# A convolutional LSTM over image diagonals followed by a small circuit layer: first statistics shared by ScalarE and Pool, the waiting rows' bias as a matmul, and diagonals declared apart from other rows

## The chip, the cores and the metric

One Trainium2 chip, one core of it. The metric is the device time of one execution in microseconds (us); the kernel before takes 1460.05 us, the median of three runs (1458.62 to 1461.36). A profiled execution adds a trace of every instruction of the engines: TensorE (PE, with its weight loads as PEld), VectorE (DVE), ScalarE (ACT), Pool (GpSimd), and the DMA queues (SP's above all).

## What is computed

The input x is 16 images of 128 channels, 64 by 64. Two layers, each with a group normalisation ahead of it and a residual around it:

```python
x = x + diagonal_lstm(group_norm(x), w_is, b_is, w_ss, b_ss)
x = x + circuit(group_norm(x), pre_w, pre_b, q_weights, post_w, post_b)

# diagonal_lstm: row i of an image is shifted right by i, so that column t of the shifted image is
# a diagonal. The scan goes over the 127 columns; all 64 rows at once, one state (h, c) per row.
gates = w_is @ xs[t] + w_ss[:, :, 0] @ h_of_the_row_above + w_ss[:, :, 1] @ h + b
o, f, i = sigmoid(gates[0:3]);  g = tanh(gates[3])
c = f * c + i * g;  h = o * tanh(c)          # h is the output for this column
```

A row whose pixels have not begun still moves on: its input is zero, and its state, the same for all images, follows from the bias and the row above. Group normalisation takes mean and variance over four channels and all pixels of an image. The second layer is per pixel: four angles from the channels, sines, amplitudes of a 4-qubit circuit, four expectations, 128 outputs.

## The kernel before

Channels lie on the 128 partitions. The kernel has three stages.

**Preparation (L220 to L430).** For each image b, `rows(b)` and `behind(b)` start the DMAs of x on SP's queue: 40 of the 64 rows go into `ring`, which stays, the other 24 into seven passing buffers. `statistics(b, k)` (L285) takes bn_stats of a chunk of 512 pixels on VectorE, eight for each image, and `aggregated(b)` (L289) joins them by bn_aggr into mean and variance `mv1`. Beside that runs the recursion of the waiting rows, `inv_step` (L191), 33 steps one after the other: four matmuls of the summed weights wsT with hinv (L199), four activations with the gate's bias (L202), two products and a sum on Pool (L205 to L207), a tanh (L209) and the product with the output gate (L210), which gives the next hinv. After each step come two matmuls by `keep` (L179), whose results nobody reads. The loop over b (L375) writes down, for each image, some two steps, then the image's DMAs, then its statistics. After it, Pool copies hinv into the scan's first state (L402, L403), TensorE multiplies it (L408) and runs three more `keep`s, the group mean and inverse root are made, and the scan's first product (L583) follows. `turned` and `coefficients` (L300, L312) make the circuit's coefficients with a sine on ScalarE and small Pool operations, early in this stage.

**Scan (L501 to L890).** 160 steps. The 64 rows are taken as 32 slots in two bands: band 0 is rows 0 to 31, band 1 follows 65 steps later with rows 32 to 63. `step(t)` (L753) multiplies on TensorE: for the state's sums and differences (L763), and `gate_ps(t + 1)` (L576) the normalised input of the next step (L583). VectorE adds (L778), ScalarE activates (L782, L842), VectorE makes the new state (L848). Pool makes the differences of neighbouring rows (`differences`, L614 and L617), adds the state of the step before to x in `ring` (`residual`, L627), and normalises the diagonal of step t + 2 (`normalised`, L564, L569, L574). Each diagonal is an access pattern over `ring` that touches one pixel of each active row in all images, so that its extent spans nearly the whole ring. `statistics(us)` (L703) takes bn_stats of finished rows on VectorE for the second layer's normalisation, as many as fit the given time. When four rows 4g to 4g + 3 are finished, with g below 6, they are stored to DRAM (`low`, L639); when their statistics are taken too, four later rows are reloaded in their place (L722). Within a step the order written is: products, statistics, residual of t - 1, normalising of t + 2, gates. Dependencies between engines and DMAs are found from the tiles and extents that instructions read and write, and turned into semaphore waits.

**Second layer (L947 to L1122).** Per image and chunk: angles, sines, amplitudes, outputs, and the store.

The order on each engine is the order in which the code is written (`manual_schedule`).

## Time and profile before

| | |
|---|---|
| median of three runs | 1460.05 us |
| the profiled execution | 1460.57 us |
| its span in the profile | 1458.5 us |
| PE busy | 1368.0 us (94%) |
| DVE busy | 972.0 us (67%) |
| POOL busy | 887.0 us (61%) |
| ACT busy | 776.8 us (53%) |
| mean granted TensorE clock | 0.982 |

The page gives busy times by engine, the span in 40 slices, the DMA queues, the chain of work that ended last, and the costliest groups of instructions. By time: the preparation lasts to about 103 us, the scan to about 1331 us, the second layer to the end. A wait is shown as the idle time of an engine ahead of an instruction and what released it ("<-POOL spare L617"). In a timeline a line begins with the start in us and the duration, and "x8" means that eight instructions are merged.

### The profile page before, as it was taken

To read this page: it belongs to the slowest core of one execution; us is meant where nothing else is said; L and a number is where in the kernel's file an instruction comes from. 1 tells how busy PE (TensorE), PEld (TensorE's weight loads), DVE (VectorE), ACT (ScalarE), POOL (GpSimd) and SP (SyncE) were. 2 spreads that over 40 slices of the span, in tenths; PEclk is the share of its full clock that TensorE was granted. 3 is DMA by queue.
4 is the path that set the end of the run, shared out by engine and by line. 5 is a ranking of instruction groups with operands and counts; after the bars stand their busy time and mean duration, and the time that the engine had idled before them with its cause. 6 is when DMAs were issued, how large, how long until landed. Compare 5 with 4: busy or idle time off the path is not lost.

```text
span 1458.5 us, 20029 instructions
## 1 busy us (share of the span) xinstructions
PE 1368.0 (94%) x6046; PEld 974.5 (67%) x6046; DVE 972.0 (67%) x2541; ACT 776.8 (53%) x1852; POOL 887.0 (61%) x1599
## 2 busy tenths in 40 slices
PE   6788999999999999988888899999999999999995
PEld 4668877776677766655555577767776677886332
DVE  7963555566665667765555667766666557776996
ACT  4555666555555555544444455555555556654331
POOL 4226777776677767566556577777777666763310
PEclk9999999999999999999999999999999999999998
DMA  9950000000000000323332200000000000003999
GB/s 341 407 199 1 2 1 1 1 0 1 1 1 1 1 0 1 116 73 101 116 116 86 87 0 1 1 1 1 1 1 1 0 1 1 1 30 120 362 404 355
DMA packets 64075, 107.04 MB, mean 73 GB/s; under 512 B 5040, under 2 KB 32720, under 8 KB 63968
## 3 DMA queue, kind: packets, MB, share of 16 engines
q1 hardware_dynamic: 59328, 94.39, 17.9%
q0 software_dynamic: 3408, 10.58, 2.0%
q8 instruction: 48, 0.79, 0.2%
q10 hardware_dynamic: 1232, 0.80, 0.2%
q14 instruction: 59, 0.48, 0.1%
HBM read 59.61 MB, written 46.14 MB: 73 GB/s over the span
## 4 chain that ended last, share of the span: by engine, by line
PE 77%; DVE 4%; DMA 3%; POOL 3%; issue 1%; ACT 1%; DVEq 0%; ACTq 0%; SPq 0%; POOLq 0%
PE ps L763 44%; PE ps L583 26%; DMA ring<-in_x_dram 3%; PE po_None L1042 3%; PE theta_None L991 2%; PE am_None L1020 1%; POOL ring L627 1%; DVE spare L848 1%; DVE stats L715 1%; DVE ps L838 1%; POOL spare L574 1%; DVE ps L778 1%; POOL spare L569 1%; DVE cst L841 0%; ACT g L842 0%
## 5 line engine op out<-in xcount | busy, mean ns | idle before, releaser
L583 PE MATMUL ps<-spare,wxT 128*128 128x512 f32 (+18 forms) x1280 | 479.6, 517 | 0.6 <-POOL spare L574 0.6
L778 DVE TENSOR_TENSOR ps<-ps,both 128x256 f32<-128x256 f32 (+9 forms) x536 | 219.9, 410 | 355.5 <-PE ps L763 350.2
L782 ACT ACTIVATE ps<-ps,bias 128x512 f32<-128x512 f32 (+23 forms) x480 | 279.3, 583 | 264.7 <-DVE ps L778 228.9
L763 PE MATMUL ps<-spare,w0T 128*128 128x256 f32 (+16 forms) x1272 | 352.3, 359 | 35.1 <-POOL spare L617 35.1
L763 PE MATMUL ps<-spare,w1T 128*128 128x256 f32 (+16 forms) x1272 | 353.2, 360 | 9.4 <-DVE spare L739 5.0
L583 PEld LDWEIGHTS ps<-spare,wxT 128*128 128x128 f32 x1280 | 231.1, 190 | 173.3 <-issue 155.5
L627 POOL TENSOR_TENSOR ring<-ring,spare 128x256 f32<-128x256 f32 (+15 forms) x375 | 231.7, 645 | 103.8 <-DMA ring<-in_x_dram 56.2
L813 ACT COPY both<-ps 128x256 f32<-128x256 f32 (+9 forms) x536 | 189.8, 356 | 181.8 <-PE ps L763 162.3
L763 PEld LDWEIGHTS ps<-spare,w0T 128*128 128x128 f32 x1272 | 234.8, 194 | 60.3 <-POOL spare L617 37.7
L763 PEld LDWEIGHTS ps<-spare,w1T 128*128 128x128 f32 x1272 | 234.8, 194 | 38.3 <-DVE spare L848 6.9
L763 PEld LDWEIGHTS ps<-spare,wsT 128*128 128x128 f32 x1088 | 196.3, 190 | 79.1 <-DVE spare L848 30.0
L763 PE MATMUL ps<-spare,wsT 128*128 128x256 f32 (+14 forms) x1088 | 243.9, 366 | 1.6 <-DVE spare L848 1.1
L574 POOL TENSOR_TENSOR spare<-spare,rstd 128x512 f32<-128x512 f32 (+10 forms) x160 | 171.0, 1069 | 14.7 <-DVE rstd L158 2.3
L569 POOL TENSOR_TENSOR spare<-ring 128x256 f32<-128x256 f32 (+13 forms) x165 | 140.1, 849 | 0.0
L842 ACT ACTIVATE g<-cst 128x256 f32<-128x256 f32 (+20 forms) x320 | 102.9, 368 | 64.8 <-DVE cst L841 64.3
L848 DVE TENSOR_TENSOR spare<-g,ps 128x256 f32<-128x256 f32 (+17 forms) x319 | 105.3, 368 | 43.2 <-ACT g L842 40.2
L564 POOL TENSOR_TENSOR spare<-ring,mean 128x256 f32<-128x256 f32 (+15 forms) x191 | 123.0, 644 | 5.6 <-DVE mean L148 5.4
L617 POOL TENSOR_TENSOR spare<-spare 128x240 f32<-128x240 f32 (+9 forms) x136 | 102.5, 754 | 33.6 <-DVE spare L848 29.8
L782 ACT ACTIVATE g<-ps,bias 128x512 f32<-128x512 f32 (+20 forms) x160 | 97.4, 609 | 31.0 <-DVE ps L778 24.7
L841 DVE TENSOR_TENSOR cst<-cst,ps 128x256 f32<-128x256 f32 (+20 forms) x320 | 104.6, 368 | 5.5
L838 DVE TENSOR_TENSOR ps<-ps,g 128x512 f32<-128x512 f32 (+20 forms) x160 | 95.0, 594 | 18.4 <-ACT g L782 18.3
L830 DVE TENSOR_TENSOR cst<-cst,ps 128x512 f32<-128x512 f32 (+20 forms) x160 | 92.8, 580 | 16.4 <-POOL spare L607 10.8
(370 smaller groups left out, 1015.7 us busy)
## 6 DMA issues: line engine op xcount, KB each, us to landing
out_dram<-ring SPq DMA_DIRECT2D x93, 256.0 KB, 5.1
ring<-in_x_dram SPq DMA_DIRECT2D x32, 512.0 KB, 7.3
low<-ring SPq DMA_DIRECT2D x6, 2048.0 KB, 7.5
ring<-in_x_dram SPq DMA_DIRECT2D x6, 2048.0 KB, 8.1
spare<-in_x_dram SPq DMA_DIRECT2D x27, 256.0 KB, 6.4
rest<-in_x_dram SPq DMA_DIRECT2D x21, 256.0 KB, 6.4
ring<-low POOLq DMA_DIRECT2D x18, 256.0 KB, 6.6
ring<-in_x_dram SPq DMA_DIRECT2D x16, 256.0 KB, 7.1
```

The costliest lines, as they stand in the source:

```text
L564: nc.gpsimd.tensor_sub(by_pairs(xn, 0, j0, j1), x0, over(mean1, j1 - j0))
L569: nc.gpsimd.tensor_sub(by_pairs(xn, 1, j0, j1), lower, of)
L574: nc.gpsimd.tensor_mul(v, v, r)
L583: nc.tensor.matmul(ps[g][:, :, a:b], lhsT=wxT[:, g * 128 : (g + 1) * 128], rhs=xns[t % 2][:, :, a:b], start=t > 0, stop=True, skip_group_c ...
L627: engine.tensor_add(x1, x1, by_pairs(new, q, j0, j1))
L763: nc.tensor.matmul(out, lhsT=w[:, g * 128 : (g + 1) * 128], rhs=rhs, start=False, stop=True, skip_group_check=True,)
L778: nc.vector.tensor_add(v, v, both[g][:, a:b])
L782: nc.scalar.activation(to[:, :, a:w], ps[g][:, :, a:w], FUNC[g], bias=bias[:, g : g + 1])
L813: nc.scalar.copy(both[g][:, a:b], ps[g][:, 0, a:b])
L838: nc.vector.tensor_mul(ig, ig, act[GG][:, :, a:w])
L841: nc.vector.tensor_add(c[:, q], c[:, q], ig[:, q])
L848: nc.vector.tensor_mul(new[:, q, a:v], th[:, q, a:v], act[GO][:, q, a:v])
```

## The change

Three things. First, for images 1 to 4 one of the eight chunks is no longer taken by bn_stats: ScalarE makes its sum and its sum of squares (`moments_of`), and for images 1 to 12 bn_aggr is replaced by small Pool operations for four images together (`gathering`), of which one or two are written down after each step of the waiting rows (`some`), and the rest after the loop. Second, `inv_step` puts the bias into PSUM by a matmul with the identity, adds the four products in the same bank, and activates three gates at once; the two `keep`s in the loop go, and the coefficients, with their sine, move behind the loop. Third, in the scan the diagonals' reads and adds are declared to have no dependency on the statistics, stores and reloads of other rows (`apart`, `ahead_of`); a band-1 diagonal that reaches the reloaded rows keeps its dependency on the reload.

```diff
@@ -26,6 +26,7 @@
 BLOCK = ROWS * NW
 CHUNK = 2 * BLOCK
 EARLY = 33
+GATHER = 4
...
-        def inv_step(j, pool):
-            ps = {}
-            rhs = hinv[:, j : j + 1].to_broadcast([P, P])
-            for g in ORDER:
-                ps[g] = pool.tile([P, P], F32, name=f"inv_ps{j}_{g}", tag=f"inv{g}")
-                w = wsT[:, g * 128 : (g + 1) * 128]
-                nc.tensor.matmul(ps[g], lhsT=w, rhs=rhs, start=True, stop=True)
+        def inv_step(j, pool, ident):
+            ps = pool.tile([P, 4, P], F32, name=f"inv_ps{j}", tag="inv")
+            of = bias.unsqueeze(2).to_broadcast([P, 4, P])
+            nc.tensor.matmul(ps, lhsT=ident, rhs=of, start=True, stop=False, skip_group_check=True)
+            for g in (GO, GF, GI, GG):
+                nc.tensor.matmul(
+                    ps[:, g],
+                    lhsT=wsT[:, g * 128 : (g + 1) * 128],
+                    rhs=hinv[:, j : j + 1].to_broadcast([P, P]),
+                    start=False,
+                    stop=True,
+                    skip_group_check=True,
+                )
             ac = small.tile([P, 4], F32, name=f"inv_a{j}", tag="inv_a")
-            for g in ORDER:
-                nc.scalar.activation(ac[:, g : g + 1], ps[g][:, 0:1], FUNC[g], bias=bias[:, g : g + 1])
+            nc.scalar.activation(ac[:, GO:GG], ps[:, GO:GG, 0], AF.Sigmoid)
+            nc.scalar.activation(ac[:, GG : GG + 1], ps[:, GG, 0:1], AF.Tanh)
...
             ps_prep = prep_ps.enter_context(tc.tile_pool(name="ps_prep", bufs=2, space=PSUM))
-            ps_inv = prep_ps.enter_context(tc.tile_pool(name="ps_inv", bufs=1, space=PSUM))
-            ps_keep = prep_ps.enter_context(tc.tile_pool(name="ps_keep", bufs=1, space=PSUM))
+            ps_inv = prep_ps.enter_context(tc.tile_pool(name="ps_inv", bufs=2, space=PSUM))
...
+            entries = stats[:, :, 0:8].rearrange("p b g (h s) -> p b (g h) s", s=3)
+            aside = range(1, 1 + GATHER)
+            sums1 = w_amp[:, 1, 0 : 2 * NB].rearrange("p (k i) -> p k i", i=NB)
+            gathered, within = (
+                w_amp[:, 0, k * P // 2 : (k + 1) * P // 2].rearrange("p (i e) -> p i e", i=GATHER)
+                for k in range(2)
+            )
+            def moments_of(b):
+                at = place(SLOTS)
+                v, x0 = ring[:, b, at : at + CHUNK], ring[:, b, at : at + 1]
+                junk = ps_small.tile([P, CHUNK], F32, name=f"junk{b}", tag="small")
+                for k, func in enumerate((AF.Identity, AF.Square)):
+                    nc.scalar.activation(
+                        junk, v, func, bias=x0, scale=-1.0, accum_out=sums1[:, k, b : b + 1]
+                    )
+                nc.scalar.activation(
+                    entries[:, b, 0:2, 1],
+                    sums1[:, 0, b : b + 1].to_broadcast([P, 2]),
+                    AF.Identity,
+                    bias=x0,
+                    scale=-1.0 / CHUNK,
+                )
+            def gathering(b0):
+                b1 = b0 + GATHER
+                pair = [P, GATHER, 2]
+                means, inners = entries[:, b0:b1, :, 1], entries[:, b0:b1, :, 2]
+                s1, s2 = (sums1[:, k, b0:b1] for k in range(2))
+                if b0 in aside:
+                    nc.gpsimd.tensor_mul(s1, s1, s1)
+                    nc.gpsimd.tensor_scalar_mul(s1, s1, -0.5 / CHUNK)
+                    yield
+                    nc.gpsimd.tensor_scalar_mul(s2, s2, 0.5)
+                    nc.gpsimd.tensor_add(
+                        inners[:, :, 0:2], *(v.unsqueeze(2).to_broadcast(pair) for v in (s1, s2))
+                    )
+                    yield
+                m, var = (mv1[:, b0:b1, k] for k in range(2))
+                def total(to, v):
+                    n = 8
+                    while n > 1:
+                        nc.gpsimd.tensor_add(gathered[:, :, 0:n], v[:, :, 0:n], v[:, :, n : 2 * n])
+                        v, n = gathered, n // 2
+                        yield
+                    nc.gpsimd.tensor_add(to.unsqueeze(2), v[:, :, 0:1], v[:, :, 1:2])
+                    nc.gpsimd.tensor_scalar_mul(to, to, 1.0 / 16)
+                    yield
+                yield from total(m, means)
+                nc.gpsimd.tensor_sub(gathered, means, m.unsqueeze(2).to_broadcast([P, GATHER, 16]))
+                nc.gpsimd.tensor_mul(gathered, gathered, gathered)
+                yield
+                nc.gpsimd.tensor_scalar_mul(within, inners, 1.0 / BLOCK)
+                nc.gpsimd.tensor_add(gathered, gathered, within)
+                yield
+                yield from total(var, gathered)
             q3 = qw.rearrange("p (n a) -> p a n", a=3)
+            warm = small.tile([P, 1], F32, name="warm0", tag="inv_t")
...
@@ -307,9 +374,10 @@
                 nc.gpsimd.tensor_scalar_mul(ang[:, 1], ang[:, 1], 1.0 / (4.0 * math.pi))
                 nc.gpsimd.tensor_scalar(rnd, ang, ROUND, ROUND, ALU.add, ALU.subtract)
                 nc.gpsimd.tensor_sub(ang, ang, rnd)
+            def coefficients():
                 nc.scalar.activation(trig, ang, AF.Sin, scale=TWO_PI)
-            def coefficients():
+                nc.scalar.activation(warm, shift, AF.Sqrt)
                 nc.gpsimd.tensor_mul(co[:, 0], trig[:, 0, 0, :], trig[:, 0, 2, :])
                 nc.gpsimd.tensor_mul(co[:, 1], trig[:, 1, 0, :], trig[:, 0, 2, :])
                 nc.gpsimd.tensor_mul(co[:, 2], trig[:, 0, 1, :], trig[:, 1, 2, :])
@@ -361,7 +429,6 @@
                 nc.vector.tensor_add(sum_n[:, 2 * i : 2 * i + 2], v[:, :, 0::2], v[:, :, 1::2])
             transposed("wsT", wsT, lambda g: sum_n[:, g, :])
             biases()
-            coefficients()
             for v in (*hst, *xns, none):
                 nc.gpsimd.memset(v, 0.0)
             nc.gpsimd.memset(w_image, 0.0)
...
             done = 0
+            behind_pool = []
+            def some():
+                for later in behind_pool[:1]:
+                    if next(later, True) is not None:
+                        behind_pool.pop(0)
             for b in range(NB):
                 while b < NB - 1 and done * (NB - 1) < EARLY * (b + 1):
-                    inv_step(done, ps_inv)
-                    keep(ps_keep, "keep", ring[:, b, CHUNK : CHUNK + P])
-                    keep(ps_keep, "keep", wsT[:, 0:P])
+                    inv_step(done, ps_inv, ident)
+                    some()
                     if done == 0:
                         transposed("wxT", wxT, lambda g: wx_n[:, g, :])
@@ -385,15 +458,25 @@
                     elif done > 4 and between:
                         between.pop(0)()
                     done += 1
+                if b in aside:
+                    moments_of(b)
                 if b + 2 < NB:
                     rows(b + 2)
                 if b + 1 < NB:
                     behind(b + 1)
                     for k in ORDERED:
-                        statistics(b + 1, k)
+                        if k or b + 1 not in aside:
+                            statistics(b + 1, k)
                 for k in (5, 6, 7):
                     statistics(b, k)
-                aggregated(b)
+                if b in (0, *range(13, NB)):
+                    aggregated(b)
+                if b in (5, 9, 13):
+                    behind_pool.append(gathering(b - GATHER))
+            for later in behind_pool:
+                for _ in later:
+                    pass
+            coefficients()
             prep_ps.close()
...
@@ -551,6 +634,18 @@
         def by_pairs(v, q, j0, j1):
             return v[:, q, j0 * NB : j1 * NB].rearrange("p (j i) -> p j i", i=NB)
+        reloads = {}
+        def apart(op, *groups):
+            for key in groups:
+                tc.declare_no_dep(op.ins, group=key, reason="other rows of the ring")
+            return op
+        def ahead_of(op, band, j1):
+            apart(op, "stores", *(f"reload{g}" for g in reloads if band == 0 or 2 * j1 <= AHEAD + 4 * g))
         def normalised(t):
...
@@ -561,12 +656,14 @@
                 j0, j1 = max(0, s0 - 1 + s0 % 2) // 2, (s1 + 1) // 2
                 if j0 < j1:
                     x0 = diagonal(t, band, 0, j0, j1)
-                    nc.gpsimd.tensor_sub(by_pairs(xn, 0, j0, j1), x0, over(mean1, j1 - j0))
+                    op = nc.gpsimd.tensor_sub(by_pairs(xn, 0, j0, j1), x0, over(mean1, j1 - j0))
+                    ahead_of(op, band, j1)
                 j0, j1 = s0 // 2, s1 // 2
                 if j0 < j1:
                     lower, upper = (diagonal(t, band, q, j0, j1) for q in (1, 0))
                     of = over(mean1, j1 - j0) if plain(t) else upper
-                    nc.gpsimd.tensor_sub(by_pairs(xn, 1, j0, j1), lower, of)
+                    op = nc.gpsimd.tensor_sub(by_pairs(xn, 1, j0, j1), lower, of)
+                    ahead_of(op, band, j1)
...
@@ -624,7 +721,9 @@
                     j0, j1 = (s0 + 1 - q) // 2, (s1 + 1 - q) // 2
                     if j0 < j1:
                         x1 = diagonal(t, band, q, j0, j1)
-                        engine.tensor_add(x1, x1, by_pairs(new, q, j0, j1))
+                        op = engine.tensor_add(x1, x1, by_pairs(new, q, j0, j1))
+                        ahead_of(apart(op, "statistics"), band, j1)
+                        tc.add_to_no_dep_group(f"residual{t}", op.ins)
             for g in range(NG2):
...
                 if done == NW:
                     if 4 * g < NLOW:
-                        nc.sync.dma_start(
+                        store = nc.sync.dma_start(
                             out=low[:, :, 4 * g * NW : (4 * g + 4) * NW].rearrange("b c n -> c b n"),
                             in_=block(4 * g),
                         )
+                        tc.add_to_no_dep_group("stores", store.ins)
...
                     v = q[:, i]
-                nc.vector.bn_stats(stats[:, i, g - FIRST * k, :], v)
+                op = nc.vector.bn_stats(stats[:, i, g - FIRST * k, :], v)
+                apart(op, *(f"residual{n}" for n in range(t + 1, now)))
+                tc.add_to_no_dep_group("statistics", op.ins)
                 if i == NB - 1:
                     if g == FIRST - 1:
                         sums.append(early_sums())
                     elif g >= FIRST:
                         sums.append(late_sums(g, k, (w1 - w0) / NW))
                     if 4 * g < NLOW:
-                        nc.sync.dma_start(
+                        reloads[g] = nc.sync.dma_start(
                             out=q,
                             in_=xv[:, :, (RING + 4 * g) * NW : (RING + 4 * g + 4) * NW].rearrange(
                                 "b c n -> c b n"
                             ),
                         )
+                        tc.add_to_no_dep_group(f"reload{g}", reloads[g].ins)
```

More of the change, by code (lines that the diff above doesn't have):

```diff
@@ L635, in residual @@
                     w0 = ends[k - 1] if k else 0
-                    waiting.extend((g, k, w0, done, i) for i in range(NB))
+                    waiting.extend((t, g, k, w0, done, i) for i in range(NB))
                 if done == NW:
                     if 4 * g < NLOW:
-                        nc.sync.dma_start(
+                        store = nc.sync.dma_start(
                             out=low[:, :, 4 * g * NW : (4 * g + 4) * NW].rearrange("b c n -> c b n"),
@@ L701, with statistics @@
         sums = []
-        def statistics(us):
+        def statistics(us, now):
             while waiting:
-                g, k, w0, w1, i = waiting[0]
+                t, g, k, w0, w1, i = waiting[0]
                 us -= 0.12 + (w1 - w0) * 0.0035
@@ L800, in step @@
             ready, sums[:] = list(sums), []
-            statistics(1.65 if w - a <= LEAST else 2.1)
+            statistics(1.65 if w - a <= LEAST else 2.1, t)
             if t:
@@ L831, in step @@
             if t > NSTEP - 4:
-                statistics(0.4)
+                statistics(0.4, t)
             add(GO)
@@ L884 @@
                 ps = step(t, ps)
-            statistics(10.0)
+            statistics(10.0, NSTEP)
             for later in sums:
```

## The prediction

> **What bounds the kernel now.** I read the chain that ended last first, then the waits of TensorE, then the waits of Pool in the stretch that the chain points at, then the timeline of one such place, and last the preparation before the scan. The chain by engine:
>
> ```profile
> PE 77%; DVE 4%; DMA 3%; POOL 3%; issue 1%; ACT 1%; DVEq 0%; ACTq 0%; SPq 0%; POOLq 0%
> ```
>
> Most of the span is TensorE working; 3% is a DMA that the chain itself waits for, `ring<-in_x_dram`. TensorE's waits between 100 and 1260 us show one entry of weight (total, times, longest):
>
> ```profile
> PE ps L763 <- POOL spare L617: 34.5, 6, 6.6
> ```
>
> and Pool's waits between 590 and 850 us say why Pool was late six times:
>
> ```profile
> POOL ring L627 <- DMA ring<-in_x_dram: 56.2, 6, 10.0
> POOL spare L868 <- DVE spare L848: 28.1, 16, 4.0
> POOL ring L627 <- DVE stats L715: 19.5, 12, 2.4
> ```
>
> L627 is the residual's add. The timeline of the first of the six:
>
> ```profile
> 608.31 1.89 PE L763 MATMUL ps<-spare,wsT 128*128 128x256 f32 x8
> ...
> 609.60 1.39 DVE L715 BATCH_NORM_STATS2 stats<-ring 128x6 f32<-128x256 f32 x4
> ...
> 611.14 0.37 SPq L722 DMA_DIRECT2D ring<-in_x_dram  x1
> ...
> 619.53 1.89 POOL L627 TENSOR_TENSOR ring<-ring,spare 128x208 f32<-128x208 f32 x4 [10.04 <-DMA ring<-in_x_dram]
> ...
> 625.84 1.22 PE L763 MATMUL ps<-spare,w0T 128*128 128x256 f32 x2 [6.60 <-POOL spare L617]
> ```
>
> The last statistics of four rows end at 610.99, the reload of their place starts at 611.14, and the residual of other rows waits until it has landed; the differences of the next step (L617) stand behind it on Pool, and TensorE stands behind those. In the preparation the reader should see one step of the waiting rows:
>
> ```profile
> 77.88 1.16 PE L199 MATMUL inv_ps<-hinv,wsT 128*128 128x128 f32 x8 [0.47 <-ACT hinv L210]
> 78.40 0.93 ACT L202 ACTIVATE inv_a<-inv_ps,bias 128x1 f32<-128x1 f32 x4 [0.58 <-PE inv_ps L199]
> ...
> 79.19 0.20 POOL L206 TENSOR_TENSOR inv_i<-inv_a 128x1 f32<-128x1 f32 x1 [0.19 <-ACT inv_a L202]
> ...
> 79.46 0.20 POOL L207 TENSOR_TENSOR cinv<-inv_i 128x1 f32<-128x1 f32 x1
> 79.56 1.27 DVE L287 BATCH_NORM_STATS2 stats<-rest 128x6 f32<-128x512 f32 x2
> 79.69 0.20 ACT L209 ACTIVATE inv_t<-cinv 128x1 f32<-128x1 f32 x1 [0.36 <-POOL cinv L207]
> ```
>
> and how the preparation ends:
>
> ```profile
> 93.80 0.37 DVE L290 BATCH_NORM_AGGREGATE mv<-stats 128x2 f32<-128x48 f32 x1
> 93.82 0.19 POOL L207 TENSOR_TENSOR cinv<-inv_i 128x1 f32<-128x1 f32 x1
> ...
> 94.28 0.29 ACT L210 ACTIVATE hinv<-inv_t,inv_a 128x1 f32<-128x1 f32 x1
> ...
> 94.99 0.49 PE L408 MATMUL ps<-spare,w1T 128*128 128x128 f32 x2 [0.83 <-POOL spare L403]
> ...
> 103.19 2.05 PE L583 MATMUL ps<-spare,wxT 128*128 128x128 f32 x16 [0.65 <-POOL spare L574]
> ```
>
> Two things end together: VectorE's statistics (94.17) and the chain of the waiting rows (94.57). The next step of that chain would have begun at 94.63. The scan's first product follows 8.2 us after the first matmul of L408.
>
> **What the skill says.** The Trainium skill, "TensorE: Matmul & The Clock Gate", Part 1: TensorE falls to half clock after an idle window of about 3.4 us, and comes back after a busy one. The trace agrees: after the stall of 6.60 us, the first pairs of matmuls stand 0.85 us apart (626.86 to 627.71), those from 629.30 on 0.43. "ScalarE: Activation LUTs", Rules for kernel authors: about 0.3 us per ACTIVATE and 0.83 ns per element, by which 512 elements are an estimated 0.72 us; the trace's own 128x512 copy (L326) took 0.57 to 0.59, so I use 0.6. No page bears on dependencies that are declared away.
>
> **Part 1, ring rows apart.** It removes the residual's wait for DMA and for statistics. A step of the scan in full width takes 8.613 us (301.47 us for 35 steps between 263.57 and 565.04). Six stalls lie between the step that starts at 599.59 and the one at 847.90: 248.31 us for 23 steps, where 23 x 8.613 = 198.10. **They cost 50.2 us**, 8.4 each: 34.5 us of idle TensorE, the rest half clock and refilling. What is late next: by the instruction order of the changed kernel, the only wait for a reload that stays is one per group, in the normalising of the step after (second part of L564). Reload: start 611.14, or 2.8 us into its step, plus 8.2 us = 11.0, or 2.4 us into the next. Pool comes to that instruction after the differences (1.2), the residual (1.9) and the first part of normalising (1.5): 4.6 us into the step. So 2.2 us are in hand, and what is normalised is multiplied only a step later. The store of the next group starts after the next residual, so it does not meet the reload. Bounds: -44 (a wait of 1 us stays in each) to -53. In the narrow last steps, residuals also wait for statistics (10.2 us of Pool's waits from 1180 to 1345), nearly all off the path: -1, bounds 0 and -3.
>
> **Part 2, a step of the waiting rows.** Asked for in narrow windows, the four activations of the step above start at 78.40, 78.63, 78.85 and 79.07, each 0.31 us after the second pass of its gate's matmul (78.09, 78.31, 78.54, 78.76): the four run as a pipeline. The path is the third one (tanh, GG), end at 79.11, Pool 79.19. After, the four products signal once, behind the fourth; by the instruction order the sigmoid waits for it and the tanh has no wait of its own. So the sigmoid starts where the fourth activation did, 79.07, the tanh one interval of 0.225 later, 79.29, instead of 78.85. **Each step is 0.445 us longer**, 2.39 to 2.83; nothing else in it changes. 32 steps (the first apart): +14.2. The two activations that go were not on the path, apart from one interval: lower bound -0.225 x 32 = -7 (if the products cost nothing), upper bound +16. The matmul with the identity (two passes of 0.43) lies between a step's products (over after 0.9 us plus a drain of 0.25) and 2.83: hidden, and it takes the place of the two `keep`s.
> At the start it is not hidden: bias is needed before it, at half clock (the first step's passes are 0.22 us apart), and in the second step it stands behind the transposes. I put the second step's products at 19.5 instead of 17.48: +2, bounds 0 and +3.
>
> **Part 3, statistics on ScalarE, combining on Pool.** VectorE loses 4 x 0.674 and 12 x 0.372 = 7.2 us. Worth nothing here: the chain of the waiting rows ends later than it. If that cover were gone, the DMA of x, busy until about 91 us, allows some 2 us. ScalarE gets 4 x (0.6 + 0.6 + 0.25); between the last activation of a step and the next sigmoid it has some 1.3 us, so each costs 0.2 to 0.3, and the one that meets the output weights about 1: +2, bounds 0 and +6.
> Pool's combining goes one or two instructions at a time into the gaps of 2 us in each step, hidden. But only 19 steps come after the first is queued, and it and the second use them up: by the instruction order **21 of these instructions stand behind the last step**, then the seven of `coefficients`, and then the copies of L402 for which TensorE waits. Price: three sums at 1.47 (32 elements 0.27, 16 0.22, below 0.19, each with 0.08 for waiting on the one before, as from 79.19 to 79.46), six of 64 elements at 0.41, coefficients 1.3, copies 0.5: 8.7 us, where it was 0.98 (94.01 to 94.99). **+7.7**, bounds +5 and +10.
> TensorE then has nothing for some 10 us, so by the page it starts at half clock: the 16 products and three `keep`s before the group mean take 4.7 us now; I add 2.5, bounds 0 and 3.4. ScalarE's sine and root tables (1.28 each) lie under Pool's row.
>
> **Sum.** Preparation: 14.2 + 2 + 2 + 7.7 + 2.5 = +28.4. Scan: -50.2 - 1. The profiled execution took 1460.57 (span 1458.5, 2.07 around it): 1460.57 + 28.4 - 51.2 = 1437.8. The median of the runs is 0.5 below that execution: **1437**.
>
> **Rivals.** (B) The steps of the waiting rows are not longer: for it, two activations fewer on the engine that Pool waits for most (48.6 us); against it, the 0.31 us between product and activation, four times the same. Then 1437 - 14 = 1423, and 1416 if they are 7 us shorter: 1420. (C) Slower: TensorE runs the waiting rows at half clock, since the `keep`s are gone. Each gate takes 0.45 instead of 0.22, the sigmoid starts 0.9 later, 32 x 0.9 = 29: 1466. It decides from where the share of streaming in a window falls below what keeps the clock; against it, that share was 12 passes of 0.11 in 2.39 (55%), and is 8 x 0.11 + 2 x 0.43 in 2.83 (61%). (D) The declarations do not do what they say, or Pool waits as long at the remaining wait: half the stalls stay, 1462. Against it, the order of instructions and the 2.2 us in hand.
>
> **How the numbers follow.** Forecast 62% (1437, itself 1428 to 1447), B 25% (1420), C 6% (1466), D 7% (1462, two parts of seven faster, two the same, three slower). Faster 0.62 + 0.25 + 0.02 = 0.89, same 0.02, slower 0.06 + 0.03 = 0.09; 0.2% is about what a measurement of this kernel can tell from no change. The range leaves out C and D and the lower edge of B: 1414 to 1448.
>
> **What would show it.** Right: no TensorE wait for L617's successor above 1 us in the scan, and steps of 8.61 throughout; 2.83 us from one step of the waiting rows to the next; a row of some 31 Pool instructions after the last of them with TensorE idle; the scan's first product at about 131 us. Wrong: steps of 2.4 or less, or Pool waiting for the reload for several us in normalising.

## The result, and the profile after

The changed kernel takes 1434.94 us (median of 4 runs, 1432.97 to 1435.29), the kernel before 1459.92 (4 runs): a ratio of 0.983, with a 95% interval from 0.981 to 0.984. The prediction was 1437. The profiled execution of after is the 1432.97 one, with a span of 1431.2.

By the two profiles the 27.3 us between the spans (1458.5 and 1431.2) are three terms. The scan's first product moved from 103.19 to 125.83 us: **+22.6**. From there to the last product with wxT it took 1224.2 us (to 1327.4) and takes 1174.8 (to 1300.6): **-49.4**. What follows is 0.5 shorter.

The chain that ended last, by engine; the DMA that had 3% of it is gone:

```profile
PE 81%; DVE 4%; ACT 1%; issue 1%; POOL 1%; DVEq 0%; ACTq 0%; POOLq 0%
```

TensorE's waits between 95 and 1240 us (total, times, longest). No entry for L714, the former L617, is left; the long wait is a new one, ahead of the scan:

```profile
PE ps L491 <- POOL spare L486: 9.5, 1, 9.5
PE ps L866 <- DVE spare L842: 5.1, 11, 1.1
...
PE ps L866 <- DVE spare L704: 1.3, 3, 0.6
```

Pool's waits between 580 and 880 us, where it used to wait for reloads and statistics. Both entries that are left are the slack of a Pool that is ahead:

```profile
POOL spare L971 <- DVE spare L951: 67.9, 31, 3.0
POOL spare L711 <- DVE spare L951: 7.4, 3, 2.6
```

The timeline around the first reload (Pool, the queue and the statistics):

```profile
632.29 1.89 POOL L724 TENSOR_TENSOR ring<-ring,spare 128x208 f32<-128x208 f32 x4
633.65 1.39 DVE L815 BATCH_NORM_STATS2 stats<-ring 128x6 f32<-128x256 f32 x4
...
635.12 0.37 SPq L824 DMA_DIRECT2D ring<-in_x_dram  x1
...
641.39 1.89 POOL L724 TENSOR_TENSOR ring<-ring,spare 128x192 f32<-128x192 f32 x4
```

The reload starts at 635.12 and lands 8.4 us later, at 643.5. The next residual (L724) runs at 641.39, while it is under way, and TensorE's waits above have no entry that stems from it. The reader can also see that the statistics (633.65) start before the residual of the same step is over.

The same step of the waiting rows as was shown of before, now 2.67 us from product to product:

```profile
77.93 1.16 PE L199 MATMUL inv_ps<-hinv,wsT 128*128 128x128 f32 x8 [0.65 <-ACT hinv L217]
...
79.13 0.17 ACT L208 ACTIVATE inv_a<-inv_ps 128x3 f32<-128x3 f32 x1 [1.25 <-PE inv_ps L199]
79.20 0.17 ACT L209 ACTIVATE inv_a<-inv_ps 128x1 f32<-128x1 f32 x1
79.38 0.19 POOL L212 TENSOR_TENSOR inv_i<-inv_a,cinv 128x1 f32<-128x1 f32 x1 [1.29 <-ACT inv_a L209]
...
79.52 0.19 POOL L213 TENSOR_TENSOR inv_i<-inv_a 128x1 f32<-128x1 f32 x1
79.79 0.19 POOL L214 TENSOR_TENSOR cinv<-inv_i 128x1 f32<-128x1 f32 x1
```

The sigmoids start 1.20 us after the first product, behind the fourth. The tanh stands only 0.07 behind them. Then two products follow on Pool, one after the other. In the kernel before the first of them needed the first activation alone, and was over (79.00) when the third activation ended (79.11):

```profile
78.81 0.19 POOL L205 TENSOR_TENSOR inv_i<-inv_a,cinv 128x1 f32<-128x1 f32 x1 [1.55 <-ACT inv_a L202]
```

And the end of the preparation (Pool's row is cut to its two ends):

```profile
107.39 0.29 ACT L217 ACTIVATE hinv<-inv_t,inv_a 128x1 f32<-128x1 f32 x1
107.58 0.32 POOL L356 TENSOR_TENSOR w_amp<-w_amp 128x64 f32<-128x64 f32 x1
...
115.48 0.18 POOL L486 COPY spare<-hinv 128x1 f32<-128x1 f32 x1
115.72 0.79 PE L491 MATMUL ps<-spare,w1T 128*128 128x128 f32 x2 [9.49 <-POOL spare L486]
116.30 0.64 PE L491 MATMUL ps<-spare,w0T 128*128 128x128 f32 x2
116.73 0.63 PE L491 MATMUL ps<-spare,w1T 128*128 128x128 f32 x2
```

TensorE waits 9.49 us, and then the pairs of L491 stand 0.43 us apart (116.30 to 116.73) where those of L408 stood 0.22 apart: half clock. Of Pool's 30 instructions in between, all but the last three belong to the sums and coefficients.

### The profile page after: what moved, and what is told of

Same layout as the page of the kernel before. It is cut to its first block, busy times and chain, and to the rows that moved or that the text cites. A ratio compares the mean times of both kernels' runs of the same rounds, so it can differ in the third digit from the quotient of the medians.

```text
span 1431.2 us, 19898 instructions
## 1 busy us (share of the span) xinstructions
PE 1360.8 (95%) x5980; PEld 958.7 (67%) x5980; DVE 971.0 (68%) x2525; ACT 761.3 (53%) x1808; POOL 896.3 (63%) x1645
## 4 chain that ended last, share of the span: by engine, by line
PE 81%; DVE 4%; ACT 1%; issue 1%; POOL 1%; DVEq 0%; ACTq 0%; POOLq 0%
PE ps L866 45%; PE ps L680 28%; PE po_None L1144 3%; PE theta_None L1093 2%; PE am_None L1122 1%; DVE spare L951 1%; DVE ps L941 1%; DVE stats L815 1%; DVE ps L881 0%; DVE cst L944 0%; ACT g L945 0%; ACT g L885 0%; ACT ps L885 0%; PE po L1144 0%; DVE ring L1162 0%
## 5 line engine op out<-in xcount | busy, mean ns | idle before, releaser
L866 PE MATMUL ps<-spare,w1T 128*128 128x256 f32 (+16 forms) x1272 | 346.8, 354 | 9.4 <-DVE spare L842 5.1
L866 PE MATMUL ps<-spare,w0T 128*128 128x256 f32 (+16 forms) x1272 | 344.0, 352 | 0.0
L866 PEld LDWEIGHTS ps<-spare,w1T 128*128 128x128 f32 x1272 | 230.6, 190 | 36.2 <-issue 7.3
L866 PEld LDWEIGHTS ps<-spare,w0T 128*128 128x128 f32 x1272 | 230.5, 190 | 21.0
L724 POOL TENSOR_TENSOR ring<-ring,spare 128x256 f32<-128x256 f32 (+15 forms) x375 | 231.2, 643 | 17.7 <-DVE spare L951 17.6
L714 POOL TENSOR_TENSOR spare<-spare 128x240 f32<-128x240 f32 (+9 forms) x136 | 102.6, 754 | 36.3 <-DVE spare L951 32.5
L971 POOL COPY spare<-spare 128x16 f32<-128x16 f32 x64 | 21.0, 328 | 151.1 <-DVE spare L951 151.1
```

Of the source, the lines that this page charges most:

```text
L724: op = engine.tensor_add(x1, x1, by_pairs(new, q, j0, j1))
L866: nc.tensor.matmul(out, lhsT=w[:, g * 128 : (g + 1) * 128], rhs=rhs, start=False, stop=True, skip_group_check=True,)
```

## The experiments

"The changed kernel" has 1434.94 us. The kernel before was measured again beside the runs that follow, in three groups, with medians of 1460.94, 1460.06 and 1461.21 us, where it had 1459.92 beside the changed kernel. So differences of about 1 us between medians of different groups are not to be read.

### What the ring's declarations are worth

One part of the change alone, on the kernel before: `apart`, `ahead_of`, and the groups of stores, reloads, residuals and statistics. The preparation is untouched.

```
 (kernel before)
+reloads = {}
+def apart(op, *groups): ...
+def ahead_of(op, band, j1): ...
-engine.tensor_add(x1, x1, by_pairs(new, q, j0, j1))
+op = engine.tensor_add(x1, x1, by_pairs(new, q, j0, j1))
+ahead_of(apart(op, "statistics"), band, j1)
+tc.add_to_no_dep_group(f"residual{t}", op.ins)
```

> Only the third part of the change, on the kernel before: the ring's rows are declared apart, the preparation stays as it was. My theory, by the two traces: the scan from its first product to its last lost 49.4 us and the preparation gave 22.6 back, each by itself. Then this kernel is 50 us below the kernel before, about 1410 us, its scan's first product stays at about 103 us, and no residual waits for a reload. Rival: the stalls went because the changed preparation also shifted when rows are summed and reloaded; then part of them comes back here and the time lies at 1425 to 1450 us.

Measured: 1411.67 us (1411.28 to 1412.93), a ratio of 0.966 (0.965 to 0.968). The scan's first product is at 103.58, and Pool's waits between 560 and 850 us are

```profile
POOL spare L888 <- DVE spare L868: 67.5, 31, 2.9
POOL spare L628 <- DVE spare L868: 4.8, 2, 2.6
```

No reload, no statistics: the 50 us are this part's, alone. What the rest of the change does is the difference to the changed kernel: 1434.94 - 1411.67 = 23.3 us of loss, which agrees with the 22.6 of the two profiles.

Which of the declarations? The changed kernel without those between residuals and statistics:

```
-ahead_of(apart(op, "statistics"), band, j1)
+ahead_of(op, band, j1)
...
-apart(op, *(f"residual{n}" for n in range(t + 1, now)))
```

> The changed kernel without the declaration between residuals and statistics; those for reloads and stores stay. Theory: the six stalls came from the reload alone; Pool waits again for statistics of up to 2.4 us, mostly inside its slack of 2 us or more in each step: 1435 to 1440 us. Rival: the wait for statistics was a part of the stalls, since a reload follows the last statistics of its rows: 10 us or more come back, 1445 or above.

Measured: 1433.75 us (1431.88 to 1435.12), no difference from the changed kernel that can be told. Pool's waits between 580 and 880 us:

```profile
POOL spare L970 <- DVE spare L950: 39.5, 28, 2.5
POOL ring L724 <- DVE stats L815: 32.3, 23, 2.4
```

The wait for statistics is back in full, 32.3 us, and the wait for the new states (67.9 in the changed kernel) has become 28.4 shorter. It is slack that changed its name. The stalls came from reloads. The declarations on the stores stayed in this run and were not taken out by themselves; in the kernel before Pool's waits name no store.

### What makes a step of the waiting rows longer

The changed kernel with the step of the kernel before:

```
-inv_step(done, ps_inv, ident)
+inv_step(done, ps_inv)
+keep(ps_keep, "keep", ring[:, b, CHUNK : CHUNK + P])
+keep(ps_keep, "keep", wsT[:, 0:P])
 (inv_step as in the kernel before: four tiles, four activations with bias)
```

> The changed kernel with the waiting rows' step of the kernel before (a tile, a product and an activation with bias for each gate, and the two keeps). By the traces a step took 2.70 us where it took 2.39: theory: 31 x 0.31 = 9.7 us come back and about 1 us at the start, 1424 us, and the interval between two activations of L217's kind is 2.39 us. If the step was as much longer as I had predicted (0.445) and something else hid a part, 14 us: 1421. Rival: the longer step is not what set the end of the preparation (Pool's row of sums would then start later for another reason): 1435, no change.

Measured: 1422.89 us (1422.15 to 1423.14), 12 less; between the two profiles the scan's first product moved by 10.0 (115.85 after 125.83). The steps are 2.39 us again; the last one ends at 96.72 + 0.29 instead of 107.39 + 0.29. Of these 10.7 us, 2.5 lie at the start (the second step's last activation is at 17.92 instead of 20.43). The other 8.2 are the 9.7 of the theory less 1.5, which the steps that meet ScalarE's moments and the output weights lose more here. The step does set the end of the preparation. But why is it longer? My prediction said: because the tanh stands behind the sigmoids. So it got a tile of its own, filled first:

```
+pt = pool.tile([P, P], F32, name=f"inv_pt{j}", tag="invt")
-for g in (GO, GF, GI, GG):
+for g in (GG, GO, GF, GI):
...
+nc.scalar.activation(ac[:, GG : GG + 1], pt[:, 0:1], AF.Tanh)
 nc.scalar.activation(ac[:, GO:GG], ps[:, GO:GG, 0], AF.Sigmoid)
```

> The changed kernel with the tanh gate in a PSUM tile of its own, filled first, so that its activation no longer stands behind the fourth product and the sigmoids. Theory: a step is long because both activations wait for the fourth product and run one after the other; now only the sigmoids are behind it, and Pool's second product starts 0.07 + 0.16 us earlier: 2.47 us a step instead of 2.70, 32 x 0.23 = 7 us less, 1428 us. Rival: a step's length is set by TensorE (bias and products, 1.9 us of passes) or by Pool, not by the tanh: 1435, no change.

Measured: 1434.71 us (1434.48 to 1436.72), nothing gained, and steps of 2.67 and 2.73 us as in the changed kernel. **The theory fell.** One step of it:

```profile
79.60 0.17 ACT L212 ACTIVATE inv_a<-inv_pt 128x1 f32<-128x1 f32 x1 [0.58 <-PE inv_pt L203]
...
80.27 0.17 ACT L213 ACTIVATE inv_a<-inv_ps 128x3 f32<-128x3 f32 x1 [0.50 <-PE inv_ps L203]
...
80.52 0.19 POOL L216 TENSOR_TENSOR inv_i<-inv_a,cinv 128x1 f32<-128x1 f32 x1 [1.29 <-ACT inv_a L213]
80.66 0.20 POOL L217 TENSOR_TENSOR inv_i<-inv_a 128x1 f32<-128x1 f32 x1
```

The tanh is now 0.67 us early, and Pool does what it did: both its products wait for the sigmoids, and the second follows the first after 0.14. So what should be early is the forget gate, whose product with the state is Pool's first:

```
-for g in (GO, GF, GI, GG):
+for k, i, g in ((0, 0, GF), (0, 1, GG), (1, 1, GI), (1, 0, GO)):
...
+nc.scalar.activation(ac[:, GF : GF + 1], two[0][:, 0, 0:1], AF.Sigmoid)
+nc.scalar.activation(ac[:, GG : GG + 1], two[0][:, 1, 0:1], AF.Tanh)
+nc.scalar.activation(ac[:, GO : GG : 2], two[1][:, :, 0], AF.Sigmoid)
```

> The changed kernel with the forget and tanh gates in one PSUM tile, filled first, and the input and output gates in a second one. By the trace of the run with the tanh's own tile, what is late behind the fourth product is not the tanh but Pool's row: forget gate times state, then input gate times tanh, 0.14 us apart, and in the kernel before the first of these was done while the third activation ran. Theory: here the first one is early again, and a step takes 2.56 us instead of 2.70; 31 x 0.14 = 4 us less, 1431 us. Rival: Pool's two products overlap so that the second sets the step either way, or a third activation takes its place: 1435.

Measured: 1429.00 us (1427.18 to 1430.08), 5.9 less, and 2.525 us a step (17 of them from 58.88 to 101.80). One step:

```profile
76.90 1.16 PE L203 MATMUL inv_p<-hinv,wsT 128*128 128x128 f32 x8 [0.50 <-ACT hinv L222]
77.65 0.17 ACT L212 ACTIVATE inv_a<-inv_p 128x1 f32<-128x1 f32 x1 [0.80 <-PE inv_p L203]
...
77.96 0.19 POOL L217 TENSOR_TENSOR inv_i<-inv_a,cinv 128x1 f32<-128x1 f32 x1 [1.48 <-ACT inv_a L213]
78.10 0.17 ACT L214 ACTIVATE inv_a<-inv_p 128x2 f32<-128x2 f32 x1 [0.21 <-PE inv_p L203]
78.35 0.19 POOL L218 TENSOR_TENSOR inv_i<-inv_a 128x1 f32<-128x1 f32 x1 [0.19 <-ACT inv_a L214]
```

L218, the second product, starts 1.45 us after the step's first matmul; in the changed kernel L213 starts 1.59 after it. The 0.14 are shown.

The mean step gained more, 0.18 (2.525 against 2.704), since the changed kernel's steps are of two kinds. In 10 of its last 18, Pool's first product starts not 0.08 us behind the end of the sigmoids (79.30 to 79.38) but 0.14 (52.24 to 52.38), and the step takes 2.73 instead of 2.67. The run with the early tanh has both kinds too, so this is not the tanh. In the kernel before the 0.14 was there as well (78.66 to 78.81), but ahead of a product that was not on the path, and so it is here (77.82 to 77.96). The short steps come where Pool had done two instructions of the sums in the step ahead, and the run without these sums, below, has none of them. Why Pool then starts sooner stays open.

One more size was disputed. I had put 0.225 us between sigmoids and tanh; the trace has 0.07. Is it the bias operand, which the new activations lack?

```
-nc.scalar.activation(ac[:, GO:GG], ps[:, GO:GG, 0], AF.Sigmoid)
+nc.scalar.activation(ac[:, GO:GG], ps[:, GO:GG, 0], AF.Sigmoid, bias=none[:, 0:1])
 (the tanh likewise)
```

> The changed kernel with a bias operand of zeros on the two activations of the step. I had put the tanh 0.225 us behind the sigmoids, the interval of the four activations before, which had a bias; the trace of the changed kernel has 0.07. Theory: the bias operand makes the difference; then a step is about 0.13 us longer here, 2.83 us, and the time 1439 us. Rival: the four activations stood 0.225 apart because each waited for its own product, and these stand 0.22 apart; a bias costs nothing: 2.70 us and 1435.

Measured: 1439.99 us (1439.65 to 1440.42), 5.0 more. The number is that of the theory, but only a part of it is what the theory says:

```profile
14.97 1.28 ACT L208 ACT_TABLE_LOAD   x1 [5.20 <-PE inv_ps L199]
...
81.61 0.26 ACT L208 ACTIVATE inv_a<-inv_ps,none 128x3 f32<-128x3 f32 x1 [1.25 <-PE inv_ps L199]
81.77 0.25 ACT L209 ACTIVATE inv_a<-inv_ps,none 128x1 f32<-128x1 f32 x1
```

An activation takes 0.26 us with the operand and 0.17 without, and the next starts 0.16 or 0.07 after it. A step is 2.80 us (17 from 66.06 to 113.68) instead of 2.70, since Pool waits for the longer sigmoids: 31 x 0.10 = 3. Another 1.7 lie at the start: the table load now comes after the wait for the products. In the two profiles a further 1.7 lie in one step, at the output weights (5.87 us instead of 4.15), where TensorE runs at half clock; variants without the operand have such a step too (see below). That the time is just the theory's is thus in part luck. Both sides were wrong on the 0.225: that was indeed the distance of the products, and the bias costs 0.09. The Trainium skill, "ScalarE: Activation LUTs", What ACT_TABLE_LOAD costs, has just this: 186 ns (and 0.83 ns per element) without such an operand, 93 ns more for each per-partition operand, and neighbours that overlap by about 93. The trace agrees within 0.03 us: 0.17 without and 0.26 with, and an overlap of 0.10 in both cases. The prediction should have used it.

### The row behind the last step, and TensorE's clock

The changed kernel with all first statistics on VectorE; coefficients still behind the last step:

```
-if b in aside:
-    moments_of(b)
...
-if b in (0, *range(13, NB)):
-    aggregated(b)
-if b in (5, 9, 13):
-    behind_pool.append(gathering(b - GATHER))
+aggregated(b)
```

> The changed kernel with all first statistics on VectorE again (no moments on ScalarE, no sums on Pool); the coefficients stay behind the last step. Theory: Pool's row behind the last step of the waiting rows falls from 8.3 us to about 3 (-5.5), ScalarE's moments no longer delay five steps (-2.2), and TensorE, idle for some 4 us instead of 9.5, comes back at a clock that costs 0 to 1.9 less: 1426 to 1428 us. VectorE's statistics then end at about 100 us, still ahead of the chain at about 105. Rival: VectorE becomes the bound of the preparation with its 7.2 us more: 1433 to 1435.

Measured: 1428.56 us (1428.20 to 1428.82), 6.4 less; in the two profiles the scan's first product moved by 4.8 (121.01 after 125.83). VectorE's last statistics, and TensorE's wait behind the last step:

```profile
91.84 1.81 DVE L293 BATCH_NORM_STATS2 stats<-spare 128x6 f32<-128x512 f32 x3
93.69 0.37 DVE L296 BATCH_NORM_AGGREGATE mv<-stats 128x2 f32<-128x48 f32 x1
...
110.33 0.80 PE L485 MATMUL ps<-spare,w1T 128*128 128x128 f32 x2 [4.83 <-POOL spare L480]
```

They end at 94.06, not at the 100 that I expected, and at 92.98 in the changed kernel: 7.2 us of work taken from VectorE moved its end by 1.1, 13 us ahead of the chain. Even the 1.1 lies within the spread: in the variants with the changed kernel's statistics the end is between 92.7 and 96.7. TensorE's wait before L485 is 4.83 us instead of 9.49, and its pairs again stand 0.43 apart. So half clock comes after 4.83 us of idling as well.

The clock by itself: nine matmuls into a tile that nobody reads fill Pool's row.

```
 coefficients()
+for _ in range(9):
+    keep(ps_small, "small", rests[NB - 2][0][:, 0 : 3 * P])
```

> The changed kernel with nine matmuls of 384 columns on TensorE behind the last step of the waiting rows, into a tile that nobody reads, so that it does not stand idle under Pool's row of sums. Theory: the matmuls of L491 then run at full clock (0.22 us a pair instead of 0.43) and the scan's first product comes 1.9 us earlier: 1433 us. Rival: the clock was not what cost it: 1435. If the nine outlast Pool's row, a part is lost again.

Measured: 1433.25 us (1431.73 to 1433.96).

```profile
118.37 0.49 PE L493 MATMUL ps<-spare,w1T 128*128 128x128 f32 x2 [1.12 <-POOL spare L488]
118.69 0.39 PE L493 MATMUL ps<-spare,w0T 128*128 128x128 f32 x2
...
126.77 1.49 PE L682 MATMUL ps<-spare,wxT 128*128 128x128 f32 x11 [0.65 <-POOL spare L673]
```

Full clock (the next pair starts at 118.92, 0.22 behind), and 8.40 us from the first of these products to the scan's first, where it was 10.11: 1.7 us, where 1.9 was expected. In its profile they are hidden by another loss: one step, at the output weights, took 6.2 us (from 34.63 to 40.85) where the changed kernel's took 4.1. TensorE waits 1.61 us there for ScalarE and then runs the step at half clock: the product with the identity takes 2.08 us. In the changed kernel's profile the same wait is as long, and the product takes 1.13. To see whether a keep prevents the slow step, one of the two was put back:

```
 inv_step(done, ps_inv, ident)
+keep(ps_keep, "keep", wsT[:, 0:P])
```

> The changed kernel with one of the two keeps back in each step of the waiting rows (the product with wsT, 0.44 us). In the traces of three variants one step, at the output weights, takes 5.3 to 6.2 us instead of 4.1, with TensorE at half clock after waiting 1.6 us. Theory: without keeps the share of streaming there is too small; with one, that step takes about 4.2 us, and the time is 1 to 2 us less, 1433 us. Rival: the keep stands ahead of the next step's bias and products and makes each step longer, 0.1 us or more: 1438 us and above.

Measured: 1432.65 us (1432.43 to 1433.44), and steps as in the changed kernel, 4.1 at that place: the rival fell, since a keep lengthens no step. Whether it prevents the slow step is not decided, because the changed kernel's own profile has none either. Three of the changed kernel's four runs lie at 1434.67 to 1435.29, the profiled one at 1432.97. That these three had the slow step fits this, and it is not shown: only the one was profiled. The half clock behind the long wait is another candidate, for it varies as much: in this run's profile the stretch from the first product behind that wait to the scan's first took 11.29 us, where it was 10.11.

### The start, and the shortest version

TensorE's first products and ScalarE's table load in the changed kernel, and then TensorE's in the kernel before:

```profile
9.75 1.28 ACT L208 ACT_TABLE_LOAD   x1
...
10.91 2.08 PE L197 MATMUL inv_ps<-bias,ident 128*128 128x512 f32 x2 [1.54 <-POOL bias L400]
...
12.78 1.92 PE L199 MATMUL inv_ps<-hinv,wsT 128*128 128x128 f32 x8
```

```profile
11.24 2.05 PE L199 MATMUL inv_ps<-hinv,wsT 128*128 128x128 f32 x8 [2.10 <-ACT bias L331]
```

The kernel with only the ring's rows apart, and the sine behind the last step:

```
 (e1_ring_alone)
-nc.scalar.activation(trig, ang, AF.Sin, scale=TWO_PI)
 def coefficients():
+    nc.scalar.activation(trig, ang, AF.Sin, scale=TWO_PI)
...
-coefficients()
...
 nc.gpsimd.tensor_copy(hst[0][:, 1, NB : NB + 1], hinv[:, EARLY : EARLY + 1])
+coefficients()
```

> The kernel before with the ring's rows apart (1411.7 us) and one more piece of the change: the sine of the angles, and Pool's coefficients from it, stand behind the last step of the waiting rows (here also behind the copies for which TensorE waits). Theory: a table load of 1.28 us leaves the path of the first steps, and nothing waits for the sine behind them: 1.6 us less, 1410 us; the second step starts about 1.6 us earlier. Rival: VectorE's statistics, which end with the chain, set the end of the preparation: 1411.7, no change.

Measured: **1408.39 us** (1407.10 to 1409.01), a ratio of 0.965 (0.963 to 0.966): the shortest of all. But not for the reason I gave. ScalarE in the kernel before, and then here:

```profile
10.38 0.24 ACT L310 ACTIVATE trig<-ang 128x48 f32<-128x48 f32 x1 [5.19 <-POOL ang L309]
10.52 0.57 ACT L326 COPY wsT<-wsT_ps 128x512 f32<-128x512 f32 x1
...
12.09 1.28 ACT L202 ACT_TABLE_LOAD   x1 [0.93 <-PE inv_ps L199]
```

```profile
9.40 0.58 ACT L326 COPY wsT<-wsT_ps 128x512 f32<-128x512 f32 x1 [4.19 <-PE wsT_ps L325]
...
10.98 1.28 ACT L202 ACT_TABLE_LOAD   x1 [0.93 <-PE inv_ps L199]
```

The table load is still in the path. What left is the sine's wait for Pool's angles, behind which the copy of wsT stood: 1.12 us. At the scan's first product the gain is 1.5 (102.04 after 103.58). The other 0.4 of it is scatter: the run with the ring's rows alone began its steps 0.36 later (19.90) than the kernel before (19.54), whose preparation it has. Another 1.1 between the spans lies in the scan, and its cause stays open. The rival fell: VectorE's statistics now end behind the chain (94.7 after 93.4), and the stretch from the first product behind the waiting rows to the scan's first is 8.20 us as before.

A last try on the chain of the waiting rows, its state formed on ScalarE:

```
 (e8_ring_and_late_sine)
+nc.scalar.activation(ig[:, 1:2], ac[:, GG : GG + 1], AF.Identity, scale=ac[:, GI : GI + 1])
+nc.scalar.activation(
+    c, cinv[:, j : j + 1], AF.Identity, scale=ac[:, GF : GF + 1], bias=ig[:, 1:2]
+)
-nc.gpsimd.tensor_mul(ig[:, 0:1], ac[:, GF : GF + 1], cinv[:, j : j + 1])
 (and the two other instructions of Pool; the gates in the order input, tanh, forget, output)
```

> The kernel with the ring's rows apart and the late sine (1408.4 us), and the state of the waiting rows formed on ScalarE instead of Pool: two activations with a scale (and a bias) for the two products and the sum, forget gate third, so that between activations and tanh no other engine is waited for. Theory: the path of a step loses the two hand-overs to Pool and back (about 0.08 and 0.2 us) and gains one activation in the row: 0.1 us a step, 3 us, 1405 us; VectorE's statistics then end behind the chain and leave no more than 3.7 us to gain. Rival: an activation that reads what the one before it wrote costs as much as the hand-over (0.29 us): 1408 to 1412.

Measured: 1412.24 us (1411.75 to 1412.72), 3.9 more: a miss. A step takes 2.525 us instead of 2.39:

```profile
80.07 0.29 ACT L206 ACTIVATE inv_i<-inv_a 128x1 f32<-128x1 f32 x1
80.27 0.24 ACT L204 ACTIVATE inv_a<-inv_ps,bias 128x1 f32<-128x1 f32 x1
80.55 0.39 ACT L208 ACTIVATE cinv<-cinv,inv_i,inv_a 128x1 f32<-128x1 f32 x1
```

The two added activations take 0.29 and 0.39 us, and the forget gate's stands behind the first of them.

## Why the prediction was right, and where its sizes were off

- **Scan, -50.2 and -1.** Right: -49.4 in the profiles, -49.3 for that part alone. Around the reloads, from 566 to 887 us, steps are 8.61 us but for three of 9.20 to 9.45 (between 618.31 and 663.43), 2.05 us together; TensorE waits there for VectorE (L704). The reload is no longer late for anything: the first landed at 643.5, and the second part of normalising came at 644.62, with 1.1 us in hand where I had 2.2. The declarations on statistics are worth nothing measurable, so the -1 for the last steps is not confirmed.
- **A step of the waiting rows, +0.445.** The term that was mis-sized: 2.704 us (18 from 58.72 to 107.39) against 2.39, +0.31, or 9.7 us in 31 steps instead of 13.8. The first half of it stood: the sigmoids wait for the fourth product, 0.225. The second half, a tanh 0.225 later, was wrong in place and size: the tanh is not on the path. In its place come Pool's first product, now in the row (+0.14), and sigmoids that are shorter without a bias (-0.09). That is +0.28, the step of 2.67; the rest is the later start of Pool in the steps of 2.73, 0.035 in the mean. Of these three the prediction had none, and the wrong tanh stood for their sum: that the term came out within 0.14 is in part luck.
- **Start, +2.** Measured +0.9 (the second step's last activation at 20.43 after 19.54), and it is the difference of two: with the late sine and the old step it was at 17.92. So the sine's leaving ScalarE's row is worth -1.6, which I had missed, and the new step costs +2.5 there, near my 2. The first product with the bias waits for Pool's bias, which comes behind the row of angles, and it stands ahead of the step's own products, which start at 12.78 instead of 11.24. The table load (9.75) runs ahead of the products here, where it ran behind them (12.09). The run with a bias of zeros, whose load stands behind them again, loses 1.7. That it is the second thing to wait for that holds the load back is my reading; no run tells it from the operand itself.
- **ScalarE's moments, +2.** The 31 steps lose 3.1 against 31 x 2.704, nearly all in five steps of 3.0 to 4.1 us, where before lost 0.65: +2.5. Without moments (all statistics on VectorE) 1.0 of it stays: it belongs to the new step at the output weights. The moments' own are three steps of 3.10 instead of 2.73, 1.1; the one that meets the output weights, priced at about 1, costs nothing (4.15 with and without). ScalarE's work for one image is 1.85 us (35.63 to 37.48), where I had 1.45: a pass takes 0.67 to 0.70, near the estimate of 0.72 that I had set aside for the copy's 0.6, and 0.19 for reading the sum follows each.
- **Pool's row, +7.7.** Right: 8.33 us from the start of the last activation to L491, where it was 0.71: +7.6.
- **Half clock, +2.5.** 1.9 in the profile (10.11 after 8.20), 1.7 when covered, 1.9 to 3.1 in the other variants with a wait (10.07 to 11.29).
- **VectorE's relief, nothing.** Right, and by a wide margin.

The preparation thus cost 22.6 instead of 28.4, a difference of 5.8: the step makes 4.5 of it, the start 1.1, the clock 0.6, and the moments take 0.5 back. The scan, with what follows it, gained 49.9 instead of 51.2. So the sum for the profiled execution, 1437.8, was 4.8 too high against 1432.97, and two errors of opposite sign are in it; that the median lies only 2 us from 1437 is because this execution is the fastest of the four. Rival B (steps not longer) fell with the steps of 2.67 and 2.73, and the run with the old step shows what they cost. Rival D (stalls half stay) fell with the run of the ring alone. What rival C feared, steps at half clock, occurs in the profiles of some variants, in one step instead of 32: up to 2 us, and not in the changed kernel's own profile. That the missing keeps are its cause is not shown.

## What to carry to other kernels

A wait that comes from overlapping extents alone, and that the data do not need, can be declared away, and is worth a look first: it was all of the gain here, and the other parts of the same change gave half of it back. When several small activations are merged into one, look at what each of them released on the next engine: the merged one releases everything late, and what was done in its shadow joins the row. And work moved to an idle engine is not free where that engine must finish it before the next stage begins.

## What the runs showed that I had not expected

- Half clock follows a TensorE wait of 4.83 us as it does one of 9.49, and can follow one of 1.61 between thinly filled steps; the same wait of 1.61 was followed by full clock in the changed kernel's profile. How long half clock lasts differed between variants of one kernel: 10.07 to 11.29 us for the same stretch that takes 8.2 to 8.4 at full clock. The Trainium skill, "TensorE: Matmul & The Clock Gate", Part 1, calls the length of the slow stretch run-variable, because the window in which activity is counted runs freely; the spread of these profiles agrees with that.
- A table load of 1.28 us waited for the products when its activation had a bias (12.09, and 14.97 in the run with a bias of zeros), and ran ahead of them (9.75) when it had none.
- Pool's waits for statistics, 32 us in sum, cost nothing that the times could tell, and its waits for reloads, 56 us in sum, cost 50: the sum of a wait says little until it is known who stands behind.
